# Pairing the Wu products of two batches and reordering the stages of a four-layer convolution kernel

## The chip, the cores and the metric

The kernel runs on one core of a Trainium2 chip. The time is the device time of one execution in microseconds; the other seven cores are idle. Five engines work from queues of their own: PE multiplies matrices, DVE and ACT do elementwise work, POOL and SP (and their DMA queues) move data. Each queue is served in order, and an instruction waits in it until what it reads has been written and what it overwrites has been read.

## The reference, cut to what matters

The input is 32 images of 8 channels, 256 x 256, float32. Four layers follow one another, each as `x = x + layer(group_norm(x))`.

```
# layer 0, on x = group_norm(input), drive = x
for _ in range(15):
    mapped = 3.9 * grid * (1 - grid)
    local = conv3x3(mapped, K_local)             # one 3x3 kernel for each channel
    grid = 0.85 * (0.7 * mapped + 0.3 * local) + 0.15 * drive
cml = clip(grid, 0.0001, 0.9999)
nca = sigmoid(Wu @ relu(conv3x3(x, Wp) + bp) + bu)          # 8 -> 128 -> 8 channels
g = sigmoid(Wg2 @ relu(conv3x3([x, cml, nca], Wg1) + bg1) + bg2)   # 24 -> 8 -> 8
out = g * cml + (1 - g) * nca
# layer 1: 3x3 convolution of x quantized to 127 steps (the scale comes from max|x| over all images)
# layer 2: 3x3 convolution.  layer 3: mean over 5x5 for each channel
```

## The kernel before, in words

**Two stages.** Layer 0 is done for all 32 images first, since the scale of layer 1 needs the largest |x| of all of them. Layers 1 to 3 follow in a second stage.

**Layer 0 has two strands.** `lattice(b, ahead)` does the 15 steps of image b. Six channels run on PE: they are held as patches of 16 x 8 pixels, 128 pixels on the partitions, and a step multiplies by a 128 x 128 matrix (L408, `patch_sb`). What a patch needs from its neighbours is copied by DMA into `rings` (56 partitions), and a product with a 56-row matrix adds it (L410, `ring_sb`). The channels go in three pairs, j = 0, 1, 2; the two ring products of a pair lie at partitions 0 and 64, so that they use different row tiles of the array and run at the same time. DVE then adds the drive (L418), ACT squares the result into the next state (L435: what the text calls a map), and `spread(i)` sends the rings of the next step on SP: 12 DMAs after the map of pair 1 (for pairs 0 and 1) and 12 after that of pair 2. The other two channels run on DVE alone, nine `tap` operations a step (L342), and their edges go as two DMAs on SP (`edges`, `strip`). The PSUM pool `ps_c` of the pairs has three buffers, so the second product of a pair needs the map of the pair before it.

**The other strand** is the generator `gated()`: relu(conv(x, Wp)), the product with Wu, and the gate. It runs over 256 groups n of eight to an image (`NCH` = 8); each group has four batches i of four products `ph` (L684, 72 rows of `im`, which six DMAs on POOL gather, L540). ACT makes `hh` of each (L689). `second()` multiplies the four `hh` of a batch by Wu (L661): each product has 32 columns and goes to another column tile of the array, so four run at once. It is called in the following batch after product j = 1. `gate(n)` is a generator as well; `pieces(batch)` takes it on by one piece in each batch from 31 batches later: loads, three runs of full products (L571), two products of 32 columns for the rows above and below (L579, `wgh_sb`) with the last full one (L583), then `pq` (L588) and, through `spare`, elementwise work on DVE.

**The order** on each engine is the order in which the program is recorded (`manual_schedule`); no scheduler changes it there. Each `yield` of `lattice` gives a number of microseconds of PE work that is to be put at this place, and each `yield` of `gated` the cost of what it has just recorded; the main loop takes pieces of `gated` until the debt `left` is paid or the batch number `place[0]` has reached the limit `place[1]`. In a step the debts are 0.8 + 0.8, 0.8 + 0.8 and 0.8 + `BLOCK - 4.0` for the three pairs (`BLOCK` = 12.6). The first of each two stands between the products of a pair and its map, the second after the map.

**Layers 1 to 3** are a pipeline over the images: in round b, layer 3 of image b - 3 is done, and beside it the preparation of the other layers (`tasks`, one list for each of eight places); then layer 2 of image b - 1 and layer 1 of image b, alternating in eight parts each (`both`). `quantize1` writes a quarter of `qh` (ACT, L765), `beside` copies the rows next to each block on SP (`qb` for layer 1, `xb2` for layer 2), and `stats_parts` gives the mean and deviation in parts: a product L109, a product L116, a square root on ACT, the end on DVE. `by_group` gives the statistics of layer 3 for each group by one product (L138).

Of the kernel before, what the change touches and what calls it, by code (L numbers as in the profile page):

```python
# [9 lines left out]
F32 = mybir.dt.float32  # L10
# [7 lines left out]
P = 128  # L18
# [3 lines left out]
RB = H // HB  # L22
HP, WP = H + 2, W + 2
NPX = RB * W
NCH = NPX // 512
# [27 lines left out]
RQ = 4  # L53
BLOCK = 12.6
STEPS = 15
# [16 lines left out]
def kernel(  # L72
# [59 lines left out]
    def by_group(psum, st):  # L132

        sel = small.tile([P, 4, 2], F32, name="sel")
        for j in range(2):
            nc.vector.tensor_scalar(sel[:, :, j], gsel_sb, st[:, j : j + 1], None, ALU.mult)
        ps = psum.tile([P, 512], F32, name="ps")
        nc.tensor.matmul(ps[:, 0:8], ones, sel.rearrange("p a b -> p (a b)"), start=True, stop=True)  # L138
        got = small.tile([P, 4, 2], F32, name="got")
        nc.vector.tensor_copy(got.rearrange("p a b -> p (a b)"), ps[:, 0:8])  # L140
        return got

# [30 lines left out]
    with ExitStack() as es:  # L173
        wt = es.enter_context(tc.tile_pool(name="wt0", bufs=1))
        imp = es.enter_context(tc.tile_pool(name="im", bufs=4))
        qp = es.enter_context(tc.tile_pool(name="quarters", bufs=2))
# [155 lines left out]
        def lattice(b, ahead):  # L332
# [30 lines left out]
            for t4 in range(TX // 4):  # L363
# [6 lines left out]
                if t4 == 4:  # L370
                    if b > 0:
                        store(b - 1)
                    place[1] = BATCHES * (b + 1) - (4 if b + 1 < B else 1)
                if t4 == 1:
# [10 lines left out]
            for i, cs in enumerate(((0, 3, 1, 4), (2, 5))):  # L385
                for c in cs:
                    nc.scalar.activation(inner(c), dr[:, c], AF.Square, bias=minus)
                spread(i)
                yield 1.5
            nc.scalar.mul(d2, d2, BETA_)  # L390
            for c in (0, 3, 1, 4, 2, 5):
# [3 lines left out]
                yield 0.8  # L395
            yield 5.5


            taps_of = (((1, 0), (1, 1)), ((1, 2), (0, 0), (0, 1)), ((0, 2), (2, 0), (2, 1), (2, 2)))
            for step in range(STEPS):  # L400
                for j in range(PAIRS):
# [42 lines left out]
                    if j == 1:  # L444
                        follow()
                    yield BLOCK - 4.0 if end else 0.8
            for t4 in range(TX // 4):
# [75 lines left out]
        def gated():  # L523
# [133 lines left out]
            def second():  # L657
                n, pn, four = late.pop()
                for hh, r in four:
                    i, q = divmod(r, 4)  # L660
                    nc.tensor.matmul(  # L661
                        pn[32 * q : 32 * q + 32, :], wu_sb[:, i, :], hh,
                        start=i == 0, stop=i == 3,
                    )
                if four[-1][1] == RB - 1:
                    close(n, pn)

            batch, quarter = 0, None
            for i in range(4):
                for _ in load(0, i):  # L670
                    pass
            yield 0
            coming = iter(())
            for n in range(B * NCH):
# [3 lines left out]
                for i in range(4):  # L678
# [3 lines left out]
                    for j in range(4):  # L682
# [4 lines left out]
                        )  # L687
                        hh = hp.tile([P, 512], F32, name="hh", bufs=6)
                        nc.scalar.activation(hh, ph, AF.Relu, bias=bp_sb)  # L689
                        four.append((hh, 4 * i + j))  # L690
                        for _ in range(3):
                            next(coming, None)
                        if j == 1 and late:
                            second()
                            yield 1.05
                        yield 0.87
# [3 lines left out]
                    if i == 1 and done:  # L700
                        keep_result()
                    yield from pieces(batch)
                    batch += 1
                    coming = load(n + 1, i) if n + 1 < B * NCH else iter(())
            second()
# [33 lines left out]
    with ExitStack() as es:  # L739
# [37 lines left out]
        xr2 = wt.tile([72, C, W + 4], F32, name="xr2")  # L777
        for t in (qh, qb, xh, xb2, xr, xr2):
            nc.gpsimd.memset(t, 0.0)

# [131 lines left out]
        def step(parts):  # L912
            return lambda: next(parts, None)
# [7 lines left out]
        with tc.manual_schedule():  # L921
            x1s[0] = load1(0)
            for b in range(B + 3):
                if b + 1 < B:
                    x1s[b + 1] = load1(b + 1)
                tasks = {i: [] for i in range(8)}
                if 2 <= b <= B + 1:
                    st3, parts3 = sums.pop(2)
                    for i in range(4):
                        tasks[i].append(step(parts3))  # L930

                    def groups():
# [12 lines left out]
                among(layer3(b - 3, ys.pop(b - 3)) if b >= 3 else iter(()), tasks)  # L945
# [159 lines left out]
```

## Time and profile before

| | |
|---|---|
| device time, three runs | 16030.44, 16057.42, 16071.58 us (median 16057.42) |
| profiled execution, device time | 16044.26 us |
| its span | 16042.5 us |
| layer 0 (0 to 13320 us): PE busy | 12532.4 us, mean granted clock 0.96 |
| change of stage (13320 to 13410 us): PE busy | 21.7 of 90 us |
| layers 1 to 3 (13410 to 15950 us): PE busy | 2370.4 of 2540 us, granted clock 0.97 |
| DVE, ACT, POOL busy over the span | 72%, 36%, 35% |
| SP in a step of the lattice | 26 DMA issues, 0.65 to 0.87 us each |

The stages were found in the table of 40 slices (the share of ACT falls from 4 to 1 tenths at slice 34) and measured with the view of busy time by stretch. One image of layer 0 takes some 413 us, from the first transpose of one image (L366) to that of the next in the timeline. A float32 product of the program is two passes in the profile, so 4096 products `ph` are 8192 records; some 5% of PE's records are missing from the trace.

### The profile page before, as it was taken

Reading aid. Unit: us, or ns where it says so; the run is one execution under the profiler, and the core shown is the slowest. Engines: PE = TensorE matmul, PEld = TensorE weight load, DVE = VectorE, ACT = ScalarE, POOL = GpSimd, SP = SyncE. Lnnn points to the kernel's source line nnn. Section 1 sums busy time; section 2 is a strip of 40 time slices with the busy share of each in tenths; the row PEclk is TensorE's granted clock in tenths of the full one; section 3 lists DMA queues with packets and bytes.
Section 4 is the critical chain, followed back from the end, with each engine's and each line's share of the span. In section 5 each row is a group of like instructions: output and inputs, shape, how many; then the busy total and the mean of one; then the engine's idle time right before and its main releaser. Section 6 shows DMA issues by size and latency. Waiting matters only on the chain. (4 is left out here: it accounts for less than half of the span.)

```text
span 16042.5 us, 158554 instructions
## 1 busy us (share of the span) xinstructions
PE 15001.2 (94%) x42888; PEld 5437.6 (34%) x42888; DVE 11572.5 (72%) x14652; ACT 5754.6 (36%) x8864; POOL 5667.6 (35%) x9558
## 2 busy tenths in 40 slices
PE   7999999999999999999999999999999997999999
PEld 2333333333333333333333333333333333333333
DVE  7777777777777777777777777777777775555554
ACT  3444444444434444444434444444444431111110
POOL 3433333333433433334433333333333332111111
PEclk9999999999999999999999999999999998999999
DMA  5666666666666666666666666566656554555554
GB/s 128 149 148 148 148 146 144 146 147 147 149 146 145 150 144 148 147 147 150 146 144 145 143 146 148 141 149 145 146 145 145 142 143 106 119 117 119 120 118 106
DMA packets 1172088, 2248.19 MB, mean 140 GB/s; under 512 B 472477, under 2 KB 676373, under 8 KB 1164949
## 3 DMA queue, kind: packets, MB, share of 16 engines
q0 software_dynamic: 734208, 1628.10, 42.8%
q1 hardware_dynamic: 437012, 609.95, 15.8%
q8 instruction: 370, 6.06, 0.2%
q14 instruction: 498, 4.07, 0.1%
HBM read 1169.35 MB, written 539.02 MB: 106 GB/s over the span
## 5 line engine op out<-in xcount | busy, mean ns | idle before, releaser
L342 DVE SCALAR_TENSOR_TENSOR acc<-strip,taps_sb,acc 128x1024 f32<-128x1024 f32 x3840 | 4925.9, 1283 | 485.2 <-DMA strip<-strip 387.4
L540 POOL DMA_DIRECT2D im<-xn_d x6144 | 3483.8, 573 | 4640.2 <-PE ph L684 3775.8
L684 PE MATMUL ph<-im,wp_sb 72*128 72x512 f32 x8192 | 4269.2, 635 | 269.3 <-ACT hh L689 126.5
L689 ACT ACTIVATE hh<-ph,bp_sb 128x512 f32<-128x512 f32 x4096 | 2758.0, 688 | 3778.2 <-PE ph L684 3726.1
L418 DVE SCALAR_TENSOR_TENSOR psc<-psc,flat 128x512 f32<-128x512 f32 x2880 | 1871.5, 693 | 2524.4 <-PE psc L410 2517.8
L408 PE MATMUL psc<-state,patch_sb 128*128 128x512 f32 x5760 | 2931.1, 623 | 163.0 <-ACT state L435 157.6
L435 ACT ACTIVATE state<-psc,minus 128x512 f32<-128x512 f32 x2688 | 1723.7, 689 | 3137.9 <-DVE psc L418 2756.2
L684 PEld LDWEIGHTS ph<-im,wp_sb 72*128 72x128 f32 x8192 | 1439.8, 195 | 2677.8 <-issue 1971.7
L410 PE MATMUL psc<-rings,ring_sb 56*128 56x512 f32 x5760 | 1805.7, 650 | 230.9 <-DMA rings<-state 212.6
L408 PEld LDWEIGHTS psc<-state,patch_sb 128*128 128x128 f32 x5760 | 1041.7, 194 | 1904.1 <-issue 1249.6
L871 PE MATMUL psv<-xr,w_sb 128*128 128x512 f32 x2560 | 1163.0, 600 | 1.3 <-DVE xr L852 1.3
L661 PE MATMUL pn<-hh,wu_sb 128*32 128x512 f32 x8192 | 1138.1, 624 | 0.0
L836 POOL DMA_DIRECT2D x_d<-x x512 | 324.9, 650 | 1944.5 <-DVE x L830 1703.1
L410 PEld LDWEIGHTS psc<-rings,ring_sb 56*128 56x128 f32 x5760 | 485.4, 187 | 1436.0 <-issue 1037.1
L571 PE MATMUL pg<-cq,wg_sb 128*128 128x512 f32 x1536 | 772.8, 642 | 0.0
L785 PE MATMUL psv<-xh,w_sb 128*128 128x512 f32 x1536 | 750.1, 627 | 9.6 <-issue 9.6
L571 PE MATMUL pg<-xq,wg_sb 128*128 128x512 f32 x1536 | 741.7, 620 | 0.0
L814 ACT ACTIVATE x<-psv,b_sb,sc 128x512 f32<-128x512 f32 x256 | 199.0, 777 | 1461.6 <-PE psv L789 1440.9
L562 POOL DMA_DIRECT2D xc<-xr_d x256 | 145.7, 569 | 1554.5 <-DVE ext L603 673.2
L871 PEld LDWEIGHTS psv<-xr,w_sb 128*128 128x128 f32 x2560 | 466.1, 189 | 610.9 <-issue 606.0
L342 DVE SCALAR_TENSOR_TENSOR acc<-strip,taps_sb,d 128x1024 f32<-128x1024 f32 x480 | 612.4, 1276 | 0.0
L891 DVE TENSOR_TENSOR y<-psv,y 128x512 f32<-128x512 f32 x256 | 177.1, 692 | 591.8 <-PE psv L871 591.8
(165 smaller groups left out, 12207.9 us busy)
## 6 DMA issues: line engine op xcount, KB each, us to landing
im<-xn_d POOLq DMA_DIRECT2D x6144, 96.6 KB, 4.4
rings<-state SPq DMA_DIRECT2D x1920, 70.1 KB
strip<-strip SPq DMA_DIRECT2D x960, 126.0 KB
rings<-state SPq DMA_DIRECT2D x1920, 35.1 KB
xn_d<-xb POOLq DMA_DIRECT2D x128, 516.0 KB, 11.3
nh_d<-nh POOLq DMA_DIRECT2D x256, 258.0 KB, 5.4
nr_d<-xb POOLq DMA_DIRECT2D x128, 516.0 KB, 7.0
xq<-nr_d POOLq DMA_DIRECT2D x128, 516.0 KB, 5.7
```

What stands on the lines that cost most here:

```text
L342: nc.vector.scalar_tensor_tensor(acc, strip[:, dy : dy + RQ, dx : dx + W], taps_sb[:, 3 * dy + dx : 3 * dy + dx + 1], d2 if dy == 1 and dx ...
L408: nc.tensor.matmul(pss[-1], patch_sb[:, c, :], inner(c), start=True, stop=False)
L410: nc.tensor.matmul(ps, ring_sb[base : base + RING, j, :], rings[i][base : base + RING, j - SETS[i][0], 0 : TX * SY].rearrange("p (x y) -> ...
L418: nc.vector.scalar_tensor_tensor(ps, ps, FLOOR, dr[:, c], ALU.max, ALU.add)
L435: nc.scalar.activation(inner(c), ps, AF.Square, bias=minus)
L540: nc.gpsimd.dma_start(im[24 * dy : 24 * dy + 24, k, 0:run], window(xn_d[b % 3], at, [[HP * WP, C], [1, 3], [1, run]]),)
L571: nc.tensor.matmul(o, wg1_sb[:, s, dx, :], src[:, :, dx : dx + W], start=s == dx == 0, stop=False,)
L661: nc.tensor.matmul(pn[32 * q : 32 * q + 32, :], wu_sb[:, i, :], hh, start=i == 0, stop=i == 3,)
L684: nc.tensor.matmul(ph.rearrange("p (k w) -> p k w", w=W), wp_sb, im[:, :, j * WP : j * WP + W], start=True, stop=True,)
L689: nc.scalar.activation(hh, ph, AF.Relu, bias=bp_sb)
L785: nc.tensor.matmul(o, w[:, dx, :], src[:, 2 * i : 2 * i + 2, dx : dx + W], start=dx == 0, stop=False,)
L871: nc.tensor.matmul(pss[k].rearrange("p (c w) -> p c w", w=W), w3_sb[:, dx, :], xr[:, k, mine, dx : dx + W], start=dx == 0, stop=stop,)
```

## The change: what it does

- `second()` is called in every other batch (i even) and does all that waits in `late`, so that eight products with Wu, of two batches, stand in a row. `hh` has 10 buffers in place of 6.
- The piece of the gate of a batch is taken after product j = 1 (just behind `second()` where that is called), not at the end of the batch.
- The loads of `im` run two batches ahead in place of three; the pool has 3 buffers in place of 4.
- In a step the debts are 0.8 + 1.6, 0.8 + 1.6 and 0.8 + `BLOCK - 5.6`, with `BLOCK` = 12.2. Ahead of the first step 11 us of other work are asked for in place of 5.5. The limit at the end of an image is 6 batches back from the next image's start, not 4; in the first image nothing of `gated` is taken before its initial rings are sent.
- Stage two: the zeroing moves from POOL to DVE and covers only border columns for `qh`, `xh` and `xr`; POOL keeps `xr2`. The statistics of layer 1 and the normalization for layer 2 come one place earlier, those of layer 3 one place later, the operand of `by_group` two places ahead of its product; the quarters of `qh` are made at places 0, 2, 2, 3 and `qb` is sent at place 3, not 4. Layer 1 follows layer 2 by two parts, and its last two parts come after layer 2.

```diff
-BLOCK = 12.6
+BLOCK = 12.2
...
             nc.vector.tensor_scalar(sel[:, :, j], gsel_sb, st[:, j : j + 1], None, ALU.mult)
+        yield None
         ps = psum.tile([P, 512], F32, name="ps")
...
-        return got
+        yield got
...
-        imp = es.enter_context(tc.tile_pool(name="im", bufs=4))
+        imp = es.enter_context(tc.tile_pool(name="im", bufs=3))
...
                     if b > 0:
                         store(b - 1)
-                    place[1] = BATCHES * (b + 1) - (4 if b + 1 < B else 1)
+                        place[1] = BATCHES * (b + 1) - (6 if b + 1 < B else 1)
...
+            if b == 0:
+                place[1] = BATCHES - 6
             nc.scalar.mul(d2, d2, BETA_)
...
-            yield 5.5
+            yield 11
...
-                    yield BLOCK - 4.0 if end else 0.8
+                    yield BLOCK - 5.6 if end else 1.6
...
             def second():
-                n, pn, four = late.pop()
-                for hh, r in four:
...
+                while late:
+                    n, pn, four = late.pop(0)
+                    for hh, r in four:
...
-            for i in range(4):
+            for i in range(3):
                 for _ in load(0, i):
                     pass
...
-                        hh = hp.tile([P, 512], F32, name="hh", bufs=6)
+                        hh = hp.tile([P, 512], F32, name="hh", bufs=10)
...
-                        if j == 1 and late:
+                        if j == 1 and i % 2 == 0 and late:
                             second()
-                            yield 1.05
+                            yield 2.1
+                        if j == 1:
+                            yield from pieces(batch)
                         yield 0.87
...
-                    yield from pieces(batch)
                     batch += 1
-                    coming = load(n + 1, i) if n + 1 < B * NCH else iter(())
+                    ahead = divmod(batch + 2, 4)
+                    coming = load(*ahead) if ahead[0] < B * NCH else iter(())
...
-        for t in (qh, qb, xh, xb2, xr, xr2):
-            nc.gpsimd.memset(t, 0.0)
+
+        for t in (qh, xh):
+            for w in (0, WP - 1):
+                nc.vector.memset(t[:, :, w : w + 1], 0.0)
+        for t in (qb, xb2):
+            nc.vector.memset(t, 0.0)
+        for k in range(2):
+            for w in (0, W + 2):
+                nc.vector.memset(xr[:, k, :, w : w + 2], 0.0)
+        nc.gpsimd.memset(xr2, 0.0)
...
+                if 1 <= b <= B:
+                    st, parts = sums.pop(1)
+                    for i in (0, 1, 1, 2):
+                        tasks[i].append(step(parts))
+                    tasks[2].append(lambda: normal2(x2s[b - 1], st))
                 if 2 <= b <= B + 1:
                     st3, parts3 = sums.pop(2)
                     for i in range(4):
-                        tasks[i].append(step(parts3))
+                        tasks[i + 1].append(step(parts3))
+                    parts4 = by_group(psum, st3)
+                    tasks[4].append(step(parts4))
 
                     def groups():
-                        gss[b - 2] = by_group(psum, st3)
-
-                    tasks[5].append(groups)
-                if 1 <= b <= B:
-                    st, parts = sums.pop(1)
-                    for i in range(4):
-                        tasks[i].append(step(parts))
-                    tasks[3].append(lambda: normal2(x2s[b - 1], st))
+                        gss[b - 2] = next(parts4)
+
+                    tasks[6].append(groups)
                 if b < B:
                     for k in range(4):
-                        tasks[k].append(lambda k=k: quantize1(b, x1s[b], k))
-                    tasks[4].append(lambda: beside(nc.sync, qb, qh, 0))
+                        tasks[(0, 2, 2, 3)[k]].append(lambda k=k: quantize1(b, x1s[b], k))
+                    tasks[3].append(lambda: beside(nc.sync, qb, qh, 0))
...
                 def both():
-                    for _ in layer2(b - 1, x2s[b - 1], bns[1]) if 1 <= b <= B else range(8):
-                        next(ones_, None)
+                    twos = layer2(b - 1, x2s[b - 1], bns[1]) if 1 <= b <= B else iter(range(8))
+                    for i, _ in enumerate(twos):
+                        if i > 1:
+                            next(ones_, None)
                         yield
+                    for _ in ones_:
+                        pass
```

More of the change, by code (lines that the diff above doesn't have):

```diff
@@ L657, in second @@
             def second():
-                n, pn, four = late.pop()
-                for hh, r in four:
[L660 to L666, printed above, removed]
+                while late:
+                    n, pn, four = late.pop(0)
+                    for hh, r in four:
+                        i, q = divmod(r, 4)
+                        nc.tensor.matmul(
+                            pn[32 * q : 32 * q + 32, :], wu_sb[:, i, :], hh,
+                            start=i == 0, stop=i == 3,
+                        )
+                    if four[-1][1] == RB - 1:
+                        close(n, pn)
             batch, quarter = 0, None
-            for i in range(4):
+            for i in range(3):
                 for _ in load(0, i):
```

## The prediction, made before the changed kernel was run

> **What bounds the kernel now.** I read the page first, then PE's timeline, PE's list of waits, and SP's and DVE's timelines at the places found.
>
> ```profile
> PE 15001.2 (94%) x42888; PEld 5437.6 (34%) x42888; DVE 11572.5 (72%) x14652; ACT 5754.6 (36%) x8864; POOL 5667.6 (35%) x9558
> PEclk9999999999999999999999999999999998999999
> ```
>
> PE is busy for 94% of both stages, so the time is PE's passes, what separates them, and PE's waits. PE's timeline around one group of Wu products (start, length, records):
>
> ```profile
> 6001.38 1.88 PE L684 MATMUL ph<-im,wp_sb 72*128 72x512 f32 x4
> 6003.19 1.07 PE L661 MATMUL pn<-hh,wu_sb 128*32 128x512 f32 x8
> 6004.19 1.12 PE L684 MATMUL ph<-im,wp_sb 72*128 72x512 f32 x2
> 6005.15 1.88 PE L408 MATMUL psc<-state,patch_sb 128*128 128x512 f32 x4
> ```
>
> Starts count here, not lengths: passes overlap. Four full passes that follow full ones start 0.429 us apart in the single records. Here four take 1.81, the group (two rounds of four tiles) 1.00, and the next two 0.96: 3.77 against 8 x 0.429 = 3.43. So a group costs 0.34 us beyond its passes: 0.09 going in, 0.05 inside, 0.09 coming out, 0.10 at the second pass after it. A pair of ring products pays the same at its edges and 0.10 inside.
>
> The first step of an image:
>
> ```profile
> 9938.81 1.12 PE L410 MATMUL psc<-rings,ring_sb 56*128 56x512 f32 x2
> 9945.01 2.04 PE L410 MATMUL psc<-rings,ring_sb 56*128 56x512 f32 x2 [5.08 <-issue]
> 9946.98 3.78 PE L684 MATMUL ph<-im,wp_sb 72*128 72x512 f32 x4
> 9950.69 1.94 PE L661 MATMUL pn<-hh,wu_sb 128*32 128x512 f32 x8
> 9952.55 3.53 PE L408 MATMUL psc<-state,patch_sb 128*128 128x512 f32 x4
> ...
> 9957.08 1.12 PE L408 MATMUL psc<-state,patch_sb 128*128 128x512 f32 x2
> 9958.73 1.13 PE L408 MATMUL psc<-state,patch_sb 128*128 128x512 f32 x2 [0.53 <-ACT state L435]
> ```
>
> A wait of 5.08 us for the rings is followed by rows at half speed: 2.04 + 3.78 + 1.94 + 3.53 = 11.29 where the same rows elsewhere take 1.13 + 1.88 + 1.07 + 1.88 = 5.96. The stall costs 5.1 + 5.3. The last line is another kind: a pair straight behind a pair waits for the map before it. PE's waits in total:
>
> ```profile
> PE psc L410 <- DMA rings<-state: 212.6, 78, 6.3
> PE psc L408 <- ACT state L435: 157.6, 289, 2.9
> PE psv L789 <- DMA qb<-qh: 123.1, 31, 13.5
> ```
>
> And in each image of the second stage:
>
> ```profile
> 14520.73 0.39 PE L138 MATMUL ps<-sel,ones 128*128 128x8 f32 x2 [1.05 <-DVE sel L136]
> ...
> 14540.20 0.61 PE L789 MATMUL psv<-qb,w_bf 72*128 72x512 bf16 x1 [5.13 <-DMA qb<-qh]
> 14540.61 4.04 PE L785 MATMUL psv<-xh,w_sb 128*128 128x512 f32 x6
> ```
>
> **What the Trainium skill says.** TensorEngine Tiling, Tiling Modes (Key Properties): "Changing tiling mode (not just tile) drains the TensorE". The trace agrees: 0.52 us from start to start at each change, 0.429 without. TensorE: Matmul & The Clock Gate, Part 1: an idle window of some 3.4 us halves PE's clock until a busy one has passed; agreed, 3.78 us for a row of 1.88 after an idle 5.08. SBUF - State Buffer, Who interferes with whom: a GpSimd operation and a DVE operation that needs the shared port block one another for the whole instruction; between the stages a DVE operation on two columns takes 11.95 us (13328.79 to 13340.74) and ends with POOL's memset.
>
> **The change part by part**, against the profiled execution (16,044.26 us, span 16,042.5), counted in the recorded order of the two kernels.
>
> *Wu and gate groups.* Runs of tiled products fall from 2848 to 2118. 512 are pairs made one: two single groups cost 0.68, a double 0.34 + 0.05 = 0.39, so 512 x 0.29 = 148. In 122 cases the gate's column products now stand directly behind Wu products (same tile width; edges saved, 0.29): 35. In 96 they stand behind ring products, from row tiles to column tiles, which the trace does not show: between 0 and 0.29 each, I take 0.19 (one change instead of two and the slow second pass): 18. Sum 201; image 0 waits for its own chain rather than PE, and the last image gets two batches more: **-190**.
>
> *More between pairs.* From the trace, by PE work between the ring products of one pair and the next of the same step: at 2.0 to 2.5 us 227 of 227 wait, 0.73 us each with the restart; at 2.5 to 3.0 us 52 of 146, 0.56; beyond, hardly. That is 166 + 29 = 195. The new order has 60 and 128 such places in 30 images: 44 + 26 = 70. **-125**.
>
> *More ahead of the first map.* The first step's rings wait 26 times in 30 images, 118 us, and 15.5 more where the profile says "issue"; with 5 us of half clock behind nearly each, 134 + 145 = 279. The new order puts 5.6 us more PE work there, about the wait. I take three quarters: **-210**. Limit 0 to -279.
>
> *What is late next.* Less work remains from pair 1's ring products to those of the next step's pair 0: 14.6 us on average where it was 16.0. The last of their twelve ring DMAs lands (from the semaphores, median by step) 18.8, 14.3, 15.4, 12.3, 16.9, 13.1, 11.4, 11.4, 15.9, 13.3, 13.4, 15.4, 14.7 and 19.3 us after pair 1. Above each step's own room that is 7.8 us an image before and 16.6 after. I take half of the 8.8 more, because the wider pairs free DVE before the map is due (two taps of 1.28 us are done by then) and because early DMA bursts get 5.6 us to drain: 4.4, and 1.4 of half clock: 5.8 x 30 = **+175**. Bounds 0 and +385 (all of it, and 4 of half clock). SP is the resource behind it: 24 issues at 0.70 with pauses and 2 strips at 0.9 are 18.6 of a step's 21 us.
>
> *Loads of im.* From the trace they land a median 32 us before use with three batches' lead; a batch is 413/32 = 12.9 us. One batch less leaves 19; the few with under 13 (some 3%, nearly all the batch behind the write of xn_d) stand elsewhere in POOL's new queue, with about 8 us to spare by count. In return the loads no longer queue behind a wait for the new image's xn_d (8.5 us of POOL at 9926). Cost 0.
>
> *Start and change of stage.* In image 0 a product waits 16.4 us for im between transposes that need nothing from it; the new order puts the transposes first: **-15**. Between the stages the DVE operation loses its 11.95 us and the x1 load (issued at 13340.65 behind POOL's memsets) goes out earlier; DVE gets two large memsets. VectorE: DVE Perf Modes (Zero memsets) prices one cycle an element, by which I estimate 4.3 and 2.2 us, partly in gaps: **-10**.
>
> *Layers 1 to 3.* `qb` is sent at about the same time (its last quarter is still DVE's next work) but first used two parts of layer 2 later, 2 x 3.4 us: the 109.6 us of steady waits go, with 5 of restarts. The wait for `sel` (45.5 less 12.9 at the first) goes with restarts: 37. The rows slowed behind the 5 us wait (4.04 for 2.74, some twenty times): 25. What comes: layer 1's last parts stand at the end and DVE does 1.32 us for each; by those rows its statistics are ready 6.5 us after layer 2, and L109 follows 2.6 + 3.4 = 6.0 us after it: 0.7 with the restart, 31 times, +22. Sum **-150**; bounds -180 and -90.
>
> Total: -190 - 125 - 210 + 175 - 15 - 10 - 150 = -525, so 15,519 against the profiled execution. The median of the runs is 13 us above that: **15,530 us**.
>
> **Rivals.** *A, the lattice's chain takes over:* ring waits at their upper bound, +385 rather than +175: 15,740. For it: slacks of 0 to 3 us in most steps, and SP near its limit. Against: most steps now wait for nothing. *B, the double group pays like two* (a weight load that cannot be hidden in the second four): 148 less, 15,680. Against: the second round inside a group starts 0.45 us after the first. *C, slower: the shorter im lead.* POOL stops for the gate's xc up to 20.4 us (waits for L603, 673 us in 79 waits), and the loads behind it start late; 26 us of lead less 20.4, 6.8 of issues and 4.4 of landing is -5.6. Each such load would cost 4 us and 5 of half clock. It decides from 525/31/9 = 1.9 late loads an image; three give +840, 16,370. Against: only two waits of PE for im in the whole trace, and the xc wait falls on few batches.
>
> **How the numbers follow.** Forecast 0.58, A 0.25, B 0.07, C 0.10. Own range of the forecast: gains at their ends give 15,320 to 15,690. The range for 8 in 10 reaches over A, 15,310 to 15,870, and leaves C out. What a measurement here can tell from none is 0.3%, 48 us. Forecast, A and B are faster by more: 0.85, with the weak end of A taken off; same 0.04; slower 0.11 (C and a rest of A).
>
> **What would show it.** Groups of 16 Wu records some 1.9 us from start to start; PE's waits for L408's map near 70 us; none for `qb` or `sel`, a new short one at L109; the first step's ring wait nearly gone, and short ring waits in later steps. It is wrong if the ring waits exceed 400 us in total, if `ph` waits for `im` more than a few times, or if the granted clock of layer 0 stays at 0.96.

## The result, and the profile after

The changed kernel takes 16068.71 us (median of 20 runs, 16025.06 to 16108.61) where the kernel before takes 16036.38 (20 runs): ratio 1.0022, 95% interval 1.0013 to 1.0032. It is 0.2% slower, where 3.3% of gain had been forecast.

First the page of the changed kernel: the engines' busy times, and the granted clock in 40 slices.

```profile
PE 14903.3 (93%) x42888; PEld 5573.4 (35%) x42888; DVE 11517.2 (72%) x14662; ACT 5716.4 (36%) x8864; POOL 5678.5 (35%) x9553
PEclk8999999999999999999999999999999998999999
```

PE is busy for less time than before, and yet the span is longer: PE waits more. The second view is PE's list of waits (sum in us, times, longest), still of the changed kernel:

```profile
PE ph L688 <- DMA im<-xn_d: 348.1, 66, 16.1
PE psc L411 <- ACT state L438: 184.6, 196, 3.3
PE ph L688 <- ACT hh L693: 167.3, 130, 5.7
PE psc L413 <- DMA rings<-state: 122.4, 60, 4.5
PE ps L109 <- DVE mv L106: 52.9, 35, 27.4
```

The waits for `qb` and `sel` have gone from the top of the list, as forecast. So is the new one at L109, though small: 30 short waits, 12.6 us, as 40.3 of the 52.9 us stood there before. The waits for the map (L438) did not fall. And the first line is new: 66 waits for `im`, 348 us, where the kernel before had two.

The last `pq` of layer 0 divides the two stages: layer 0 ends at 13,513 us (before: 13,320), and the rest takes 2,560 (before: 2,722). So the second stage gained 162 us and layer 0 lost 193. Layer 0 can be split further: its length, less the sum of PE's idle times in the records, less what the clock records lose to half clock (the time in which PE is busy at half clock, times one half), leaves PE's own work. Counted by line, no record of PE is missing in layer 0 (`ph` has its 8192, the patch and ring products have 5760 each), unlike the 5% given above, so the idle times are real ones.

| layer 0, us | length | PE idle | lost to half clock | own work |
|---|---|---|---|---|
| before | 13,320 | 788 | 471 | 12,062 |
| changed | 13,513 | 1,038 | 655 | 11,820 |

The change does save 241 us of PE's own work. But PE waits 250 us more than before, and half clock costs 184 us more, so layer 0 loses 193 in sum.

Where they are: all but some 10 us of the waits for `im` lie 10 to 50 us after the first transposes of an image, in two waits in nearly every image. PE's timeline there, in image 30 of the changed kernel (start, length, records, and in brackets the idle time and what ended it):

```profile
12579.62 1.88 PE L688 MATMUL ph<-im,wp_sb 72*128 72x512 f32 x4
12585.01 3.75 PE L688 MATMUL ph<-im,wp_sb 72*128 72x512 f32 x4 [3.51 <-ACT d L393]
12588.69 3.41 PE L665 MATMUL pn<-hh,wu_sb 128*32 128x512 f32 x16
...
12599.87 1.88 PE L688 MATMUL ph<-im,wp_sb 72*128 72x512 f32 x4
12606.88 2.04 PE L688 MATMUL ph<-im,wp_sb 72*128 72x512 f32 x2 [5.13 <-DMA im<-xn_d]
12608.71 3.62 PE L411 MATMUL psc<-state,patch_sb 128*128 128x512 f32 x4
```

Two stalls, each followed by rows at half speed (3.75 and 3.62 where a full row of four takes 1.88). The profile puts the first down to ACT, but it too is a wait for `im`: by the semaphores, the last of the six loads of this batch lands at 12584.87, just before PE goes on. The rings of the first step no longer wait, but the first ring product comes 49 us after the first transpose (median; 27.7 before). POOL's timeline at the same place:

```profile
12559.86 6.08 POOL L543 DMA_DIRECT2D im<-xn_d  x3 [0.49 <-DMA im<-xn_d]
12565.93 2.40 POOL L357 DMA_DIRECT2D xn_d<-xb  x4
12568.31 0.60 POOL L648 DMA_DIRECT2D nh_d<-nh  x1
12568.91 1.68 POOL L543 DMA_DIRECT2D im<-xn_d  x3
12573.15 0.56 POOL L543 DMA_DIRECT2D im<-xn_d  x1 [2.56 <-DMA xn_d<-xb]
12576.06 0.57 POOL L543 DMA_DIRECT2D im<-xn_d  x1 [2.36 <-DMA xn_d<-xb]
12580.91 0.56 POOL L543 DMA_DIRECT2D im<-xn_d  x1 [4.28 <-DMA xn_d<-xb]
12581.56 0.73 POOL L481 DMA_DIRECT2D cr_d<-xb  x1
...
12592.14 0.60 POOL L621 DMA_DIRECT2D x_d<-xc  x1 [1.95 <-DMA cr_d<-xb]
12597.66 0.56 POOL L565 DMA_DIRECT2D xc<-xr_d  x1 [4.93 <-DMA x_d<-xc]
12598.23 5.06 POOL L543 DMA_DIRECT2D im<-xn_d  x9
```

Counted from the start, the loads at 12573 to 12581 are the last three of the six of batch 956, the 29th of image 29. They read that image's `xn_d` and need nothing of the one that is written for image 30 at 12565.93, but POOL issues each only when one of these writes has landed. Nine loads more stand behind `cr_d`, `x_d` and `xc` until 12598.23: among them batch 958, for which PE waits at 12606.88.

Why a load waits for a write that it does not need can be read from the semaphores. The 9536 DMAs of POOL use eight semaphores in strict turn, 1192 times each. Most issues wait on the very semaphore that they will use (7941 name it, for the others it was free already), and none begins before the DMA eight places earlier has landed. So at most eight are under way at once. Three loads of an image are now issued eight places behind writes of `xn_d`, and that makes this line of POOL's list of waits:

```profile
POOL im L543 <- DMA xn_d<-xb: 347.1, 99, 7.6
```

Of these 99 waits 98 are for the write eight places earlier. In the kernel before none is: its 35 waits of this name (252.6 us) are for a write at most seven places earlier, 31 of them five places, the wait for the new image's `xn_d` that the prediction names. The bound itself stands there too, with 811 waits of POOL in layer 0 (977 us) that end with the landing of the DMA eight places earlier.

### The profile page after: what moved, and what is told of

Read it like the earlier page. It is cut to its first block, busy times and chain, and to the rows that moved or that the text cites. A ratio compares the mean times of both kernels' runs of the same rounds, so it can differ in the third digit from the quotient of the medians.

```text
span 16073.5 us, 157050 instructions
## 1 busy us (share of the span) xinstructions
PE 14903.3 (93%) x42888; PEld 5573.4 (35%) x42888; DVE 11517.2 (72%) x14662; ACT 5716.4 (36%) x8864; POOL 5678.5 (35%) x9553
## 5 line engine op out<-in xcount | busy, mean ns | idle before, releaser
L693 ACT ACTIVATE hh<-ph,bp_sb 128x512 f32<-128x512 f32 x4096 | 2724.4, 688 | 3518.0 <-PE ph L688 3488.7
L411 PE MATMUL psc<-state,patch_sb 128*128 128x512 f32 x5760 | 2887.9, 617 | 213.2 <-ACT state L438 184.6
L438 ACT ACTIVATE state<-psc,minus 128x512 f32<-128x512 f32 x2688 | 1718.3, 688 | 3008.1 <-DVE psc L421 2507.6
L688 PEld LDWEIGHTS ph<-im,wp_sb 72*128 72x128 f32 x8192 | 1479.9, 197 | 2865.4 <-issue 2231.9
L411 PEld LDWEIGHTS psc<-state,patch_sb 128*128 128x128 f32 x5760 | 1074.6, 195 | 1852.6 <-issue 1304.4
L850 POOL DMA_DIRECT2D x_d<-x x512 | 364.5, 727 | 1406.0 <-DVE x L844 1171.8
L799 PE MATMUL psv<-xh,w_sb 128*128 128x512 f32 x1536 | 713.3, 600 | 32.4 <-ACT x L828 26.1
L574 PE MATMUL pg<-xq,wg_sb 128*128 128x512 f32 x1536 | 703.6, 593 | 0.0
L432 DVE SCALAR_TENSOR_TENSOR strip<-acc 128x1024 f32<-128x1024 f32 x448 | 549.7, 1227 | 15.3
L574 PE MATMUL pg<-nq,wg_sb 128*128 128x512 f32 x1024 | 552.9, 667 | 0.0
```

Of the source, the lines that this page charges most:

```text
L411: nc.tensor.matmul(pss[-1], patch_sb[:, c, :], inner(c), start=True, stop=False)
L438: nc.scalar.activation(inner(c), ps, AF.Square, bias=minus)
L574: nc.tensor.matmul(o, wg1_sb[:, s, dx, :], src[:, :, dx : dx + W], start=s == dx == 0, stop=False,)
L688: nc.tensor.matmul(ph.rearrange("p (k w) -> p k w", w=W), wp_sb, im[:, :, j * WP : j * WP + W], start=True, stop=True,)
L799: nc.tensor.matmul(o, w[:, dx, :], src[:, 2 * i : 2 * i + 2, dx : dx + W], start=dx == 0, stop=False,)
```

## The experiments

All ratios are to the kernel before on the same chip, with 95% intervals; 0.1% is 16 us. Differences in the text are those of the ratios. The expectations often give differences of median times, which are some us off them, as the kernel before took from 16,036 to 16,073 us on the chips used.

### The lead of im, and POOL's queue

The kernel before with two edits of three lines, buffers and lead:

```diff
-        imp = es.enter_context(tc.tile_pool(name="im", bufs=4))
+        imp = es.enter_context(tc.tile_pool(name="im", bufs=3))
...
+                    ahead = divmod(batch + 2, 4)
+                    coming = load(*ahead) if ahead[0] < B * NCH else iter(())
```

> The kernel before with one edit: loads of im two batches ahead, three buffers. Theory: the lead alone costs most of 490 us; ph waits for im at the image starts, 300 us or more, and the time is 16,300 to 16,550 us (ratio 1.016 to 1.032). Rival (the lead hurts only together with the new order of the first step, which spends the batches that used to be in hand): ratio below 1.006.

Measured: 1.0036 (1.0024 to 1.0047), 58 us. The waits for `im` appeared, 216 us in 33 waits, and the waits for rings fell from 213 to 33. On the old order, then, the short lead mostly moves the stall of the first step to another place. The cost lies in the rival's range; the stall is of the kind that the theory named, but smaller than its 300 us.

In the changed kernel, a fourth `im` buffer does not fit beside ten `hh`. Room was made by one buffer for `above` and `below` and by loading them in a later piece of the gate:

```diff
-                    halos[n // 2] = [qp.tile([72, 4, WP], F32, name=i) for i in ("above", "below")]
-                    for q, t in ((0, nr_d), (24, cr_d), (48, nh_d)):
-                        beside_blocks(halos[n // 2], t[b % 3], q, k0)
...
                 for _ in range(4):
                     yield 0
+                if r2 % 2 == 0:
+                    halos[n // 2] = [
+                        qp.tile([72, 4, WP], F32, name=i, bufs=1) for i in ("above", "below")
+                    ]
+                    for q, t in ((0, nr_d), (24, cr_d), (48, nh_d)):
+                        beside_blocks(halos[n // 2], t[b % 3], q, k0)
```

with `bufs=4`, four first loads and `divmod(batch + 3, 4)`:

> The changed kernel with im three batches ahead and four buffers; the room comes from above and below, which get one buffer each in place of two and are loaded four batches later (one batch behind the last use of the pair before, three ahead of their own). Theory (the short lead is what the image start loses): waits of ph for im fall from 348 us to under 40, layer 0 from 13,513 to about 13,050, and the time to 15,560 to 15,680 us (ratio 0.970 to 0.978). Rival (the image start only shifts a loss: what no longer waits for im waits for the rings or the map at the first steps, as the run with the short lead alone suggests, where 216 us of im waits stood beside 180 us less of ring waits and the time rose by only 58 us): layer 0 stays above 13,300 and the time above 15,860 us.

and, as a control, without these three (the lead stays two):

> The changed kernel with only the one buffer for above and below and their later loads, im two batches ahead as changed. Control for the run with three batches: every theory expects no change against the changed kernel, 16,069 us within 50 (ratio 1.002 within 0.003). If the later loads crowd POOL or come late for the gate's column products, it is slower by up to 100 us.

Measured: 0.9819 (0.9804 to 0.9833) with the lead of three, 1.0061 (1.0044 to 1.0078) with two. They differ in the lead (with its buffers) alone: 2.4%, 388 us. With three, PE's waits read:

```profile
PE psc L411 <- ACT state L438: 174.7, 185, 2.9
PE psc L413 <- DMA rings<-state: 173.4, 98, 4.6
PE ph L691 <- ACT hh L696: 143.3, 134, 5.0
PE ps L109 <- DVE mv L106: 52.7, 35, 27.5
PE ph L691 <- DMA im<-xn_d: 50.1, 15, 15.3
```

and with two:

```profile
PE ph L691 <- DMA im<-xn_d: 405.5, 66, 16.8
```

The waits for `im` fall to 50 us, 15 of them in the first image, and the lead is shown to be a cause. The time was still 76 us above the expected range: the rings took a part (173 us for the 122 of the changed kernel). In the control the later loads of `above` and `below` cost 63 us and the waits for `im` rise from 348 to 406, which is the case that its expectation named last. So the room has a price, which the kernel before was asked for as well (the same edit on it, lead three, no other):

> The kernel before with only one buffer for above and below and their later loads: the price of making room. On the changed kernel this cost 88 us, all in image starts, where POOL's queue is late. Theory (with im three batches ahead there is room for it): within 40 us of the kernel before, ratio 1.000 to 1.0025, so that the groups alone are worth 95 to 135 us, less than the 190 of the forecast. Rival (it costs the same whatever the lead): ratio 1.005, and the groups are worth their 190.

Measured: 0.9915 (0.9901 to 0.9930), 136 us *faster*. Neither theory: on the kernel before, the waits for rings fell from 213 to 143 us and those of `ph` for `hh` from 127 to 55. So the later loads are a gain of their own on the kernel before, with its lead of three, and a loss on the changed one with a lead of two; whether the lead or the order makes the difference was not run. If that gain is the same on the changed kernel with a lead of three, that kernel without the later loads would stand at 0.9819 + 0.0085 = 0.9904, and the lead of two would cost it 1.2%, about 190 us. That kernel does not fit and was not run.

The other way to show the cause is to leave the lead and to clear the queue. Only the four writes of `xn_d` are issued by SP in the first of these runs, those of `cr_d` as well in the second (`nc.gpsimd.dma_start` becomes `nc.sync.dma_start`):

> The changed kernel, lead of two kept, with the four writes of xn_d issued by SP instead of POOL. Theory (POOL's queue behind these writes makes im late): PE's waits for im fall from 348 us to under 150 and the time to 15,650 to 15,850 us (ratio 0.976 to 0.988); the rest is the writes of cr_d, which stay on POOL. Rival (the bytes, 2 MB at once on the DMA engines, delay im whoever issues them): the waits stay above 280 us and the time above 15,980 us.

> The changed kernel as it is (im two batches ahead), with the four writes of xn_d and the four of cr_d at each image start on SP. If POOL's queue behind these writes is the whole cause of the late im: its waits fall from 348 us to under 60 and the time to 15,700 to 15,850. If the lead itself is too short (the first batches of an image cannot be loaded before xn_d has landed, whoever issues the write): im waits of 120 us or more and 15,930 to 16,000.

Measured: 0.9965 (0.9952 to 0.9977) and 0.9843 (0.9815 to 0.9871). The waits for `im` fell from 348 us to 179 and 82, and the second run gains 1.8%, 287 us, with the lead of two. The first run lies between its theory and its rival, so the writes of `xn_d` on POOL are not the whole cause; the second is in its theory's range in time, and just outside it in its waits (82 us for under 60). Of the waits that are left, 60 of the 82 us lie 30 to 40 us into an image.

The rival of the first run, the bytes, is not out. A load of `im` that is issued in the 12 us after the first write of `xn_d` of an image lands 15.0 us after its issue in the changed kernel (median, from the semaphores), where the median of all loads is 4.2. With all these writes on SP it is still 9.5 us. So part of the delay stays when POOL's queue is rid of the writes; that the bytes make it is likely, but no run separates the two.

### Layers 1 to 3

The kernel before with only the edits of the second stage:

> The kernel before with only the edits of layers 1 to 3 and of the zeroing. The forecast priced them at -160 us and the stage's share of the two traces says -162: 15,875 us, ratio 0.990. Rival (layer 0 ends in another state, so part of the 162 us belongs to the changed layer 0): ratio 0.994 or more.

Measured: 0.9895 (0.9878 to 0.9912), 168 us; layer 0 of that run ends at 13,290 and the rest takes 2,559 us, as in the changed kernel. The stage is worth what was forecast, and is independent of layer 0.

### The paired groups

The kernel before with the paired `second()`, ten `hh`, and the gate's piece behind product j = 1; lead three, with the later loads for room, so the run to compare with is the one at 0.9915:

> The kernel before with only the paired Wu groups and the gate's piece behind product j = 1 (hh with ten buffers, room from one buffer each for above and below), im three batches ahead, steps and stages as before. Forecast's term: -190 us, 15,850 us, ratio 0.988. Rival (longer stretches between products with Wu and pieces of uneven length delay the lattice or the relu of hh, and eat half of it): ratio 0.993 to 1.0.

Measured: 0.9951 (0.9936 to 0.9966). The groups make that kernel *slower*, by 0.36%, some 58 us (by the two intervals 24 to 92). Pairing and the move of the gate's piece were not run apart, so "groups" stands for both here. The two splits that belong together (the profiled execution of the run with groups is 38 us above that run's median, the other is at its median):

| layer 0, us | length | PE idle | half clock | own work |
|---|---|---|---|---|
| before, later loads | 13,185 | 646 | 483 | 12,056 |
| the same with groups | 13,265 | 862 | 586 | 11,817 |

PE's own work falls by 239 us: the groups save at least what they were priced at. 215 us come back as waits and 104 as half clock. Where they come from shows in DVE's timeline of the run with groups, at one of 60 map waits of 1.4 to 2.2 us:

```profile
7490.38 5.24 DVE L342 SCALAR_TENSOR_TENSOR acc<-strip,taps_sb,acc 128x1024 f32<-128x1024 f32 x4
7495.66 0.75 DVE L428 TENSOR_SCALAR acc<-acc 128x1024 f32<-128x1024 f32 x1
7496.44 1.23 DVE L429 SCALAR_TENSOR_TENSOR strip<-acc 128x1024 f32<-128x1024 f32 x1
7497.58 0.68 DVE L610 TENSOR_TENSOR cq<-cq,nq 128x512 f32<-128x512 f32 x1
...
7501.67 0.68 DVE L606 TENSOR_REDUCE ext<-xc 128x1 f32<-128x512 f32 x1
7502.27 1.29 DVE L418 SCALAR_TENSOR_TENSOR psc<-psc,flat 128x512 f32<-128x512 f32 x2
```

and PE's at the same time:

```profile
7499.62 1.13 PE L410 MATMUL psc<-rings,ring_sb 56*128 56x512 f32 x4
7500.68 1.13 PE L408 MATMUL psc<-state,patch_sb 128*128 128x512 f32 x2
7503.73 1.12 PE L408 MATMUL psc<-state,patch_sb 128*128 128x512 f32 x2 [1.92 <-ACT state L435]
```

DVE does not stop from 7490.4 to 7502.3: four taps, two operations for the new strip, seven of the gate's elementwise ones. PE's ring products of pair 0 are done at 7500.7, their evacuation (L418) starts only behind the last of the seven, the map follows it, and PE's second product of the next pair waits 1.92 us for the map. PE's list names ACT, but ACT only passes the delay on. DVE is busy for 76% of layer 0; in this part of a step it is busy for all of it, and the faster PE arrives sooner at a queue that has not become shorter.

So the elementwise operations were spread over the step:

```diff
                     if end:
-                        work(4)
+                        work(2)
                     else:
+                        work(1)
                         next(ahead, None)
```

first on the changed kernel with the lead of three (0.9819), then on the kernel before with later loads, with the groups and without (the 259 us of the second expectation count half clock during waits as well; the table above has 239):

> The kernel with im three batches ahead (and one buffer for above and below), with the gate's elementwise operations on DVE spread over the step: one behind pair 0's map, one behind pair 1's, two behind pair 2's, in place of four behind pair 2's. Theory (PE's remaining waits for the map come from DVE: between pair 2 and the next step's pair 0 DVE has 9.8 us of work where the narrower block leaves PE less, so pair 0's evacuation stands behind the last of the four; 98 of the 175 us of map waits follow such an operation): map waits fall from 175 to about 90 us and the time by 60 to 150 us against the same kernel without it, to 15,600 to 15,700. Rival (DVE then holds up pairs 1 and 2 as much): within 30 us of 15,756.

> The kernel before with one buffer for above and below, the paired groups, and the gate's elementwise operations spread over the step (1, 1 and 2 behind the maps of pairs 0, 1 and 2). Theory (the paired groups save 259 us of PE's own time, and DVE's queue between pair 2 and the next pair 0 turns it into waits and half clock): the spread gives back 100 to 200 us, 15,760 to 15,860, and it stands 60 to 150 us below the same kernel without the groups. Rival (the lumps of the groups themselves, up to 4.5 us of work in a row, delay the map and the relu of hh): within 50 us of the run without the spread, 15,963.

> Control: the kernel before with one buffer for above and below and the spread, no groups. Theory: only 27 us of its map waits stand behind the last of the four elementwise operations, so the spread brings little: 15,870 to 15,925 against 15,923. Rival (DVE's queue is what paces the steps of any order): 100 us or more, as for the changed order.

Measured: 0.9739 (0.9715 to 0.9763), 0.9906 (0.9891 to 0.9921) and 0.9920 (0.9903 to 0.9938). The spread is worth 128 us to the changed kernel with the lead of three, where the waits for the map fall from 175 to 89 us:

```profile
PE psc L411 <- ACT state L438: 89.2, 156, 2.7
```

It is worth 72 us where only the groups were added, short of the 100 to 200 expected, and nothing, within the interval, to the order without them (its map waits were 155 and are 146). That is the pattern expected if the saved time runs into DVE's queue. But it is not the whole of it: with the spread the groups are worth only 22 us (less than the intervals can tell from none). Their own work falls by 199 us (12,035 to 11,836), and the waits still rise by 222. The largest part is here, in PE's waits of the run with groups and spread:

```profile
PE ph L689 <- ACT hh L694: 229.9, 146, 5.3
PE psc L408 <- ACT state L435: 218.7, 430, 2.6
PE psc L410 <- DMA rings<-state: 165.1, 58, 7.2
```

In 127 of these 146 waits for `hh` the relu stood on ACT behind a map, which waited for an evacuation on DVE; in 110 of them that evacuation stood on DVE behind an operation of the statistics that come once an image (mean, deviation, peak). This is read from the trace; no run took these operations away.

### The debts and the start

The changed kernel with the lead of three, with the debts of a step as before:

```diff
-BLOCK = 12.2
+BLOCK = 12.6
...
-                    yield BLOCK - 5.6 if end else 1.6
+                    yield BLOCK - 4.0 if end else 0.8
```

> The kernel with im three batches ahead, with the debts of the step as in the kernel before (0.8 + 0.8, 0.8 + 0.8, 0.8 + 8.6). The forecast's terms: -125 for more between pairs against +175 for the rings of the next step, so 50 us faster than with the new debts, 15,706. Rival (the paired groups come in larger lumps, which alone raise the map waits from 158 to 279 us; the wider debts are what takes that back): map waits rise from 175 to about 280 us and the time by 30 to 100 us, to 15,790 to 15,860.

Measured: 0.9818 (0.9802 to 0.9835), the same as with the new debts (0.9819). The parts moved as the rival said: map waits 254 us for 175, and waits for `hh` 274 for 143, against 93 for 173 on the rings. But half clock is 448 us where the new debts have 593. So in layer 0 the new debts take out 117 us of waits and 32 of own work, and give 146 back in half clock: fewer waits (581 for 868 of over 0.15 us), but longer ones. In time neither the forecast nor the rival was right.

Last, all edits with the lead of three, the spread, and `xn_d` written by SP; and the same with the old debts and the old 5.5 us ahead of the first map:

> All edits of the change, im three batches ahead (one buffer for above and below), the spread on DVE and the writes of xn_d on SP. If the gains of the last two (132 and 81 us) add up: 15,530 to 15,570. If both remove the same waits: about 15,620.

> The same with the debts of the step and the 5.5 us ahead of the first map as in the kernel before. Forecast: +125 - 175 for the debts, +210 for the start, so 160 us slower than with the new ones. Theory from the runs (the debts are worth nothing; the start only moves the place of a wait): within 50 us of it.

Measured: 0.9697 (0.9682 to 0.9712) and 0.9712 (0.9696 to 0.9728). Debts and start together are worth 24 us (less than the intervals can tell from none), where the forecast has 160.

### A version that beats both

Between the lead of three alone and the last kernels stands the one with `xn_d` on SP and without the spread:

> The kernel with im three batches ahead, and the writes of xn_d on SP. If what is left at the image start (37.8 us from the first transpose to the first ring product, some 33 by PE's work alone) is still POOL's queue, 4 us of each image go with restarts, about 100 to 150 us: 15,610 to 15,660. If it is not, within 40 us of 15,756; if SP's issues delay the first rings, slower.

Measured: 0.9764 (0.9750 to 0.9779), 88 us, somewhat less than expected; with the spread's 128 this adds up to within 20 us of the 196 that both bring. Two more runs have `cr_d` on SP as well, with leads of three and two:

> All edits of the change, im three batches ahead, one buffer for above and below with later loads, the spread on DVE, and the writes of both xn_d and cr_d on SP. The writes of cr_d stand behind those of xn_d in POOL's queue: without them 0 to 60 us less than with xn_d alone moved, 15,490 to 15,555. If SP's queue delays the edges or first rings, slower than that by up to 50.

> The same with im two batches ahead and three buffers. If POOL's queue was the cause, the lead no longer matters with the writes off POOL: within 60 us. If the lead itself is short, 250 us or more slower, with im waits above 200 us.

Measured: 0.9682 (0.9657 to 0.9707), 15,553.69 us, no different from 15,554.17 without it, and 0.9873 (0.9841 to 0.9904). So even with the large writes off POOL, the lead of two costs 307 us. POOL's timeline of the second at one image start:

```profile
8225.98 0.56 POOL L563 DMA_DIRECT2D xc<-xr_d  x1 [8.49 <-DMA x_d<-xc]
8226.53 0.58 POOL L498 DMA_DIRECT2D above<-nr_d  x1
...
8231.93 0.55 POOL L503 DMA_DIRECT2D below<-zero  x1 [0.30 <-DMA above<-nr_d]
8232.80 1.09 POOL L544 DMA_DIRECT2D im<-xn_d  x2 [0.32 <-issue]
```

The loads of `im` now stand behind the wait for `xc` (8.49 us) and the nine loads of `above` and `below`. It is the same queue with other work in it; the later place of these nine loads belongs to the edit that makes room. PE waits here until 8242.33, just after the sixth of the loads that begin at 8232.80 has landed (8242.19 by the semaphores), and 217 of this run's 243 us of waits for `im` lie 30 to 40 us into an image, as this one does. Both edits, the lead and the writes on SP, answer one cause: a load that is issued in order on a queue with stalls of 8 us and more needs a lead that covers them, or a queue without them. The fastest kernels here, at 15,554 us, are 3.0 to 3.2% faster than the kernel before. One more run, the changed kernel with the old start (5.5 us and the limit of 4), leaves out some part of the computation, and which one is open; its time is not used. So the new start was not measured apart from the debts.

## Why the prediction was wrong

- **"Loads of im ... Cost 0": wrong, the first of two failures.** The step counted a median landing of 32 us before use, took away one batch, and left "about 8 us to spare by count" for the few loads behind the write of `xn_d`. It counted issues, not the waits between them: in the trace above three of the loads wait 2.56 + 2.36 + 4.28 us for writes to land that they don't depend on, since each stands eight places behind one. That each DMA of POOL waits for the eighth before it was to be read from the trace of the kernel before. The median said nothing, because the late loads are the same few in every image. The lead was also not alone: on the old order it costs 58 us, since the stall stands where the first step's rings waited anyway. With the lead back and room made, the changed kernel gains 388 us; about 190 of it is the lead on the kernel as changed, if the room's own effect carries over. Rival C had named the resource (POOL's queue, its stops for `xc`, though not those for the writes) and the form (late loads, 4 us and half clock) and had the chance of 0.10; it put 9 us on each late load, and the two late loads of an image cost 6 to 13 us together (190 to 388 over 31 images).
- **"Wu and gate groups: -190": right as PE's own work, wrong as time.** The double group takes 1.86 us from start to start (1.9 forecast; rival B is out), and own work falls by 199 to 239 us. In time it was between -22 and +58. The step added up what PE saves and let nothing else pace the step, although DVE is busy for 75% of layer 0 in the trace of the kernel before. DVE's queue between the evacuation of pair 2 and that of the next pair 0 is 9.8 us and more, in order; the forecast had counted DVE as freed by the wider pairs.
- **"More between pairs: -125" against "what is late next: +175": nothing in place of +50.** By the runs with old and new debts, 79 us less waiting for the map and 81 more for rings, so both had the right sign and a size too large. In the changed kernel itself the count of places did not carry over: 175 to 185 us of waits for the map remained, not 70. A part of them comes from evacuations that are late on DVE, since the spread takes out 86 of 175 us. The term that was missing is half clock, 146 us.
- **"More ahead of the first map: -210": right as to the wait, wrong as to the time.** The rings of the first step no longer wait, but with the debts this is worth 24 us in the kernel where all else is mended. Taken out, that wait leaves others: in the first 60 us of the images after the first, PE waited 181 us in sum before, 118 of them for rings, and waits 137 us in the run at 0.9819 (which has the lead and the room as well), none of them for these rings.
- **Layers 1 to 3 and the change of stage: -160, right.** 162 us in the two traces, 168 (interval 141 to 196) by itself. Here PE waited for one named transfer, the work ahead of it was counted, and no other engine was near its limit (DVE, the next, was busy for 1454 of 2540 us before). The two large memsets on DVE take 3.50 and 1.78 us, less than the 4.3 and 2.2 estimated.

The miss of 539 us is then about 190 for the lead and about 350 for gains in layer 0 that were summed but not paid out: the changed kernel with the lead of three and without the room's effect is put at 0.9904, and the kernel with the second stage's edits alone stands at 0.9895, so that on this assumption the other edits of layer 0 come to nothing. Two of the forecast's own signs of being wrong came: `ph` waits for `im` 66 times, and the granted clock of layer 0, 0.96 before, did not rise but fell to 0.94. With the three mends 15,554 us were reached, close to the forecast, but by edits that the change does not have and not by the forecast's terms: there the debts and the start bring 24 us, not 160.

## What to carry to other kernels

A saving on the busiest engine is worth time only up to the next in-order queue: before adding it up, lay the other engines' work of the same stretch (not of the whole span) end to end and see whether it still fits. The lead of a prefetch has to cover the longest stall of the queue that issues it, waits included, and that is read at the few places where stalls stand, not from a median. Where a queue's DMAs take a fixed number of semaphores in turn, look at what stands that many places ahead of each load: a large write there delays it, needed or not. When waits are traded, compare idle time and half clock together, because fewer and longer waits can cost more.

## What the runs showed of the hardware

- **Short waits cost clock.** The Trainium skill (TensorE: Matmul & The Clock Gate, Part 1) has the clock halve after at least one idle window of some 3.4 us. In layer 0 of the changed kernel 209 stretches run at half clock (137 before), each 3.41 us long or a whole multiple of it, 7.4 us on average. Of the waits that begin at full clock, 12 of 321 of 0.15 to 1 us have such a stretch begin during them or within 3.41 us after them, 53 of 100 of 1 to 2 us, 60 of 72 of 2 to 3 us, and 93 of 95 longer ones; at a moment taken at random it would be some 5%. That the waits start the stretches isn't shown by an edit, but the measurement counts against using 3.4 us as a safe bound.
- **A DMA issue can wait for another's data.** POOL's loads waited for the landing of earlier writes on the same queue that they don't depend on, up to 4.28 us each in the lines above. This comes from the program, which gives POOL's DMAs eight semaphores in turn; that the chip would have it so is not shown. SP takes longer to issue the same four writes (5.69 us in the last run, where POOL took 2.40 in the changed kernel), but POOL's loads then don't stand behind them.
- **Loads beside large writes land late.** Loads of `im` that are issued beside the writes of `xn_d` land after 9.5 us when SP issues the writes and after 15.0 when POOL does, where the median of all loads is 4.2 to 4.4.
- **Row tiles straight to column tiles** cost one change, not two: 519 ns from the ring products to the gate's column products, in line with the 0.52 us of each change before, and 409 ns from Wu products to column products, no more than a full pass.
